# Product 5 of the first layer split into seven products of its blocks, in a routed expert kernel

## The chip, the cores and the metric

The kernel runs on one core of a Trainium2 chip. The metric is the time of one execution on the device in microseconds (us), as the median of several runs.

## The reference, cut to what matters

A token mixture with eight experts. `x` has 4096 tokens of 512 numbers. Each token is rotated by a fixed 4 x 4 mixing of its four quarters (a product of two normalized quaternions and a spectral gate, which here only scales), routed to its two best experts, and each expert takes up to 1024 tokens:

```python
de = disp.reshape(E, cap, Dm)                                   # E = 8, cap = 1024, Dm = 512
h = jax.nn.relu(jnp.einsum('ecd,ehd->ech', de, fc1_w) + fc1_b)  # H = 2048
eo = jnp.einsum('ech,ehd->ecd', h, fc2_w) + fc2_b
gathered = eo.reshape(E * cap, Dm)[flat_idx]
out = jnp.sum(gathered * (gates * w)[:, :, None], axis=1)
x = x + out                                                     # added to the input
```

All arithmetic of the two layers is in float32.

## The kernel before, in words

**Stages.** A routing stage computes the choice of experts and the slot tables (about the first 45 us). Then the experts follow, each in four groups of 512 hidden units: group k is quarter g = k mod 4 of expert e = k div 4, so there are 32 groups.

**First layer.** Each group is a product of a 512 x 512 block of w1 with the expert's 512 x 1024 rotated inputs. Both factors are halved in both directions, and the product is formed in Winograd's form of Strassen's scheme, with seven products, numbered 0 to 6, instead of eight. The sums of w1's blocks are made on GpSimd (`left1`, lines 137 to 140: s0 to s3), those of the inputs once per expert, also on GpSimd (`sums`, lines 125 to 128, tiles x0 to x3). Factor 5 on the left is s1, factor 4 is s0, factor 2 is s3.

Products 1, 2, 3, 4 and 6 are split a second time in the same form: `left_sub` makes four more 128 x 128 sums on GpSimd for each of them and each group (lines 155 to 158, tiles sub), `right_sub` four more on VectorE for each of them and each expert (lines 170 to 173, tiles xsub). `within` (line 840) is one matmul of 128 x 128 with 256 columns on one such block; a product takes seven. Products 0 and 5 are not split: `half` (line 861) uses two matmuls of 512 columns for each half m, so a product takes four. A float32 matmul is two instructions in the profile.

Results land in PSUM banks (`bank1`, four of them in rotation) and are added by VectorE into four SBUF tiles, h11, h22, h21 and r12, which lie side by side in `beside`. A block that is wanted in two outputs is added to both at once. ACT copies the first results with the bias and applies the final relu. The last block of the chain is closed by `chain`: three sums of these tiles on VectorE at once (lines 827 to 829) and a fourth (`last`, line 824) as soon as product 2 of the group before has freed its tile.

**Second layer.** One step behind, the hidden units of the group before are multiplied with w2 in the same seven-product form, once for each pair of slot tiles (`st0` 0 and 2); `product2` (line 800) is eight instructions of 256 columns. VectorE adds each into the accumulator `acc` (lines 1239 to 1291); the first sum of each goes to a tile v1 of its own pool. GpSimd makes w2's sums (`right2`, tiles t).

**Order.** Nothing is scheduled automatically: the instructions stand in each engine's queue in the order in which the Python code emits them. The first layer is a generator that yields 14 times in a group, the second one also 14 times, and the driver takes one step of each in turn, so that a step of the first layer stands between two of the second on TensorE. The step number within the group, `i`, is called turn here. At each turn the driver emits further work: `later(steps, turns)` puts sums at given turns, `TURN_OF_SUM` the four sums s of the next group's weights (s2 at turn 8, s0 at 11, s1 at 12, s3 at 13), `fill_n` the four x sums of the next expert at turns 10 to 13 of g = 3. Two lists hold work without a fixed turn: `background` (VectorE's rotation of the next expert's inputs, lines 727 and 771; the stores of a finished expert, which are an ACT scaling, a GpSimd addition, line 673, and a scatter, line 657) and `fetches` (gathers on GpSimd's queue, lines 601, 633 and 694, and the exchanges of gathered inputs on SP's queue, line 707). The table `PACE` says how many of each are emitted after each step.

**Buffers that matter here.** The tiles s0 to s3 and the sub tiles exist once: the sum for the next group can be written only when TensorE has done the last matmul that reads the old one. GpSimd works strictly in its queue's order, and so do VectorE and TensorE's matmuls.

**Start.** The output is first filled with x by a DMA of 8 MB from ACT's queue (line 1155), during group 0; the expert results are later gathered from it, added to, and scattered back. Group 0 has a plain first layer without the seven-product form.

## Time and profile before

| | |
|---|---|
| median of 3 runs | 1560.28 us (1560.1 to 1561.2) |
| profiled execution | 1562.67 us, span of the trace 1560.9 us |
| TensorE matmul busy | 1522.0 us, 98% |
| VectorE busy | 1237.8 us, 79% |
| GpSimd busy | 1105.4 us, 71% |
| ACT busy | 332.0 us, 21% |
| mean granted TensorE clock | 0.987 |

The span runs from the first to the last instruction of the profiled execution. In the rows of the trace, PE is TensorE's matmuls, PEld its weight loads, DVE VectorE, POOL GpSimd, SPq the DMA queue of SyncE. A row in order of time has its start, its duration, engine, line, operation, output and inputs, shape and count; in brackets, how long the engine was idle before it and what ended that. TensorE's matmuls overlap, so that the time of one is best read from start to start.

### The profile page before, as it was taken

Reading aid. Unit: us, or ns where it says so; the run is one execution under the profiler, and the core shown is the slowest. Engines: PE = TensorE matmul, PEld = TensorE weight load, DVE = VectorE, ACT = ScalarE, POOL = GpSimd, SP = SyncE. Lnnn points to the kernel's source line nnn. Section 1 sums busy time; section 2 is a strip of 40 time slices with the busy share of each in tenths; the row PEclk is TensorE's granted clock in tenths of the full one; section 3 lists DMA queues with packets and bytes.
Section 4 is the critical chain, followed back from the end, with each engine's and each line's share of the span. In section 5 each row is a group of like instructions: output and inputs, shape, how many; then the busy total and the mean of one; then the engine's idle time right before and its main releaser. Section 6 shows DMA issues by size and latency. Waiting matters only on the chain.

```text
span 1560.9 us, 18187 instructions
## 1 busy us (share of the span) xinstructions
PE 1522.0 (98%) x6585; PEld 1220.2 (78%) x6585; DVE 1237.8 (79%) x1733; ACT 332.0 (21%) x477; POOL 1105.4 (71%) x1253
## 2 busy tenths in 40 slices
PE   5898999999999999999999999999999999999997
PEld 3676888877778878788887778887777887888886
DVE  6586888788977888688896889878898788866656
ACT  3221212221122211221113121222112221121110
POOL 1755678857898379984799567885778847987453
PEclk7899999999999999999999999999999999999999
DMA  8463104521235113440145210452123511321021
GB/s 326 159 214 94 55 28 142 148 68 55 74 115 161 36 55 113 133 140 28 38 132 157 86 54 28 142 149 68 55 70 113 142 58 55 113 96 67 1 81 53
DMA packets 79378, 152.23 MB, mean 98 GB/s; under 512 B 12022, under 2 KB 40950, under 8 KB 74168
## 3 DMA queue, kind: packets, MB, share of 16 engines
q1 hardware_dynamic: 56848, 90.24, 18.3%
q0 software_dynamic: 18048, 52.31, 11.1%
q10 hardware_dynamic: 4392, 8.52, 1.4%
q8 instruction: 52, 0.85, 0.2%
q14 instruction: 38, 0.31, 0.1%
HBM read 119.77 MB, written 25.23 MB: 93 GB/s over the span
## 4 chain that ended last, share of the span: by engine, by line
PE 88%; DVE 5%; DMA 2%; SPq 2%; POOL 1%; another core or an unknown queue 1%; issue 1%; POOLq 0%; DVEq 0%
PE a L800 26%; PE b L800 20%; PE t L840 17%; PE a L861 13%; PE u L840 7%; PE b L840 3%; PE a L840 2%; DMA xb<-in_xt_dram 1%; SPq L707 1%; PE p L992 1%; DVE xsub L173 1%; DVE beside L891 1%; DVE beside L901 0%; DMA xa<-in_xq_dram,slot_tok 0%
## 5 line engine op out<-in xcount | busy, mean ns | idle before, releaser
L836 ACT ACTIVATE beside<-beside 128x1024 f32<-128x1024 f32 x93 | 98.4, 1058 | 727.9 <-DVE beside L891 507.8
L800 PE MATMUL a<-t,beside 128*128 128x256 f32 x1024 | 242.0, 379 | 0.1
L800 PEld LDWEIGHTS a<-t,beside 128*128 128x128 f32 x1024 | 194.5, 190 | 39.7 <-issue 14.4
L891 DVE TENSOR_TENSOR beside<-t,beside 128x512 f32<-128x512 f32 x248 | 170.4, 687 | 68.9 <-PE t L840 57.3
L840 PE MATMUL t<-xsub,sub 128*128 128x256 f32 x682 | 180.0, 383 | 0.9 <-DVE beside L891 0.8
L840 PEld LDWEIGHTS t<-xsub,sub 128*128 128x128 f32 x682 | 126.8, 190 | 24.3 <-DVE beside L901 4.5
L861 PE MATMUL a<-x,s 128*128 128x512 f32 x248 | 118.4, 600 | 5.1 <-POOL s L138 5.1
L800 PE MATMUL b<-w,beside 128*128 128x256 f32 x512 | 121.0, 379 | 0.6 <-DVE acc L1284 0.6
L800 PE MATMUL a<-t,hidden 128*128 128x256 f32 x512 | 121.0, 379 | 0.0
L800 PE MATMUL a<-w,beside 128*128 128x256 f32 x512 | 120.9, 379 | 0.0
L800 PE MATMUL b<-w,hidden 128*128 128x256 f32 x504 | 119.7, 380 | 0.0
L800 PE MATMUL b<-t,hidden 128*128 128x256 f32 x504 | 119.1, 379 | 0.0
L800 PEld LDWEIGHTS b<-w,beside 128*128 128x128 f32 x512 | 97.2, 190 | 27.3 <-issue 15.8
L800 PEld LDWEIGHTS a<-w,beside 128*128 128x128 f32 x512 | 97.3, 190 | 26.4 <-issue 14.8
L800 PEld LDWEIGHTS b<-w,hidden 128*128 128x128 f32 x504 | 96.3, 191 | 26.5 <-issue 13.2
L861 PE MATMUL a<-xa,w 128*128 128x512 f32 x248 | 116.4, 592 | 0.0
L137 POOL TENSOR_TENSOR s<-w 128x512 f32<-128x512 f32 x31 | 39.5, 1276 | 106.7 <-PE t L840 106.7
L800 PEld LDWEIGHTS a<-t,hidden 128*128 128x128 f32 x512 | 97.3, 190 | 13.2
L800 PEld LDWEIGHTS b<-t,hidden 128*128 128x128 f32 x504 | 95.8, 190 | 13.0
L901 DVE TENSOR_TENSOR beside<-t,beside 128x512 f32<-128x512 f32 x124 | 85.1, 686 | 17.5 <-PE t L840 13.8
L657 POOL DMA_INDIRECT out_dram<-rows,slot_add x64 | 71.4, 1116 | 36.9 <-DVE rows L652 17.5
L140 POOL TENSOR_TENSOR s<-w,s 128x512 f32<-128x512 f32 x31 | 40.3, 1299 | 66.8 <-PE t L840 66.6
(231 smaller groups left out, 3178.5 us busy)
## 6 DMA issues: line engine op xcount, KB each, us to landing
w<-in_w_dram SPq DMA_DIRECT2D x64, 1024.0 KB
xb<-in_xt_dram SPq DMA_DIRECT2D x8, 1024.0 KB
out_dram<-in_x_dram ACTq DMA_DIRECT2D x1, 8192.0 KB
rows<-xa SPq DMA_DIRECT2D x112, 64.0 KB
rows<-xb SPq DMA_DIRECT2D x224, 32.0 KB
b<-in_b_dram POOLq DMA_DIRECT2D x8, 256.0 KB
c<-choice,slot_cho POOLq DMA_INDIRECT x64
rows<-out_dram,slot_tok POOLq DMA_INDIRECT x64
```

Source lines behind the costliest of these rows:

```text
L137: lambda: G.tensor_tensor(s[0], w[:, 1, 0], w[:, 1, 1], ALU.add),
L140: lambda: G.tensor_tensor(s[3], w[:, 0, 1], s[1], ALU.subtract),
L173: lambda: V.tensor_tensor(t[:, 3], b(1, 0), t[:, 1], ALU.subtract),
L657: nc.gpsimd.indirect_dma_start(out=out_of[st], out_offset=bass.IndirectOffsetOnAxis(ap=slot_add[:, s : s + 1], axis=0), in_=self.rows[st], ...
L707: nc.sync.dma_start(slots_of[half][q * CW : (q + 1) * CW, at : at + t.shape[1], b * P : (b + 1) * P], t[b * CW : (b + 1) * CW, :, q * P : ...
L800: nc.tensor.matmul(out[m] if isinstance(out, list) else out[:, m], lhsT=factors[0][n][:, c, (st0 + m) * P : (st0 + m + 1) * P], rhs=factor ...
L836: nc.scalar.activation(h, h, AF.Relu)
L840: nc.tensor.matmul(out, lhsT=subs[0][n][i], rhs=subs[1][n][i], start=first, stop=True, skip_group_check=True,)
L861: nc.tensor.matmul(out, lhsT=factors[0][n][:, c, m * P : (m + 1) * P], rhs=factors[1][n][:, c, :], start=first and c == 0, stop=c == 1, sk ...
L891: V.tensor_tensor(to, bank.rearrange("p (n s) -> p n s", n=2), to, ALU.add)
L901: V.tensor_tensor(to, term.unsqueeze(1).to_broadcast([P, 2, HS]), to, ALU.add)
L992: nc.tensor.matmul(ps[n][m][:, at], lhsT=w[:, block, i // 2, i % 2, m * P : (m + 1) * P], rhs=x.of(half, i)[:, at], start=i == 0 and at.st ...
```

## The change

Product 5 is split like the others. Its seven block products have four turns to themselves (3 to 6, with the start in turn 2), and their results are added by VectorE to r12 alone: four blocks to one place each, one block to two. h21, which holds r12's values with another bias, is then carried over: half 0 as the sum of product 6's block, the bias difference `b1_over` and r12 on VectorE, half 1 by ACT from r12. All later steps move on by one or two turns, products 1 and 4 overlap, and the turns for the sums and the table PACE are set anew. The sums of product 5 and product 4 on the left share one tile (sub4). The tile v1 is given up: its sum goes to a part of `acc`. The 8 MB copy to the output is issued at group 1, turn 13.

```diff
-    def left_sub(k, n, block):
+    def left_sub(k, n, block, tag=None):
...
-        t = wsum.tile([P, 4, P], F32, tag=f"sub{n}", name=f"sub{n}_{k}")
+        t = wsum.tile([P, 4, P], F32, tag=f"sub{tag or n}", name=f"sub{n}_{k}")
...
+    b1_over = const.tile([P, E, NG, 2], F32, name="b1_over")
+    by_half = b1_sb.rearrange("p e (g a m) -> p e g a m", a=2, m=2)
+    nc.gpsimd.tensor_tensor(b1_over, by_half[:, :, :, 1], by_half[:, :, :, 0], ALU.subtract)
...
-        for m in range(2):
-            half(a[m], m, 5, False)
-            nc.scalar.activation(r12[:, m], a[m], AF.Identity, bias=lo[:, m : m + 1])
             if m == 1:
-                nc.scalar.activation(h21[:, m], a[m], AF.Identity, bias=hi[:, m : m + 1])
+                nc.scalar.activation(r12[:, m], a[m], AF.Identity, bias=lo[:, m : m + 1])
...
+        t5 = bank1(f"t5_{k}")
+        singles(a[0], 5)
+        nc.scalar.activation(r12[:, 0], a[0], AF.Identity, bias=lo[:, 0:1])
+        within(t5[:, A], subs, 5, 0, True)
+        yield
+        within(t5[:, B], subs, 5, 4)
+        add_once(r12[:, 0, A], t5[:, A])
+        yield
+        within(t5[:, A], subs, 5, 5)
+        add_once(r12[:, 0, B], t5[:, A])
+        add_once(r12[:, :, B], t5[:, B].unsqueeze(1).to_broadcast([P, 2, HS]))
+        yield
+
+        u = bank1(f"u1_{k}")
+        within(t5[:, A], subs, 5, 6)
+        add_once(r12[:, 1, B], t5[:, A])
+        singles(u, 6, True)
+        V.scalar_tensor_tensor(h21[:, 0], u, over[:, 0:1], r12[:, 0], ALU.add, ALU.add)
+        yield
+        t = bank1(f"t1_{k}")
+        within(t5[:, A], subs, 5, 3)
+        add_once(r12[:, 1, A], t5[:, A])
+        nc.scalar.activation(h21[:, 1], r12[:, 1], AF.Identity, bias=over[:, 1:2])
...
             if k:
+                lefts[5], more = left_sub(k, 5, left_f[5], 4)
+                later(more, (0, 0, 1, 1))
                 for n, block, turns in (
-                    (4, left_f[4], (2, 2, 3, 3)),
-                    (2, left_f[2], (4, 4, 5, 5)),
-                    (3, w1_of[k][:, 1, 1], (6, 6, 7, 7)),
+                    (2, left_f[2], (2, 2, 3, 4)),
+                    (3, w1_of[k][:, 1, 1], (6, 7, 7, 8)),
                 ):
...
                     for n, turns in (
-                        (6, (2, 2, 3, 3)),
-                        (4, (3, 4, 4, 5)),
-                        (2, (2, 4, 7, 10)),
-                        (3, (3, 5, 8, 10)),
+                        (5, (1, 2, 3, 4)),
+                        (6, (4, 5, 5, 7)),
+                        (4, (7, 7, 9, 9)),
+                        (2, (7, 8, 9, 11)),
+                        (3, (8, 9, 11, 12)),
                     ):
...
+                    if i == 5:
+                        its[4], more = left_sub(k, 4, left_f[4])
+                        later(more, (5, 5, 6, 6))
...
+                if k == 1 and i == 13:
+
                     nc.scalar.dma_start(*(a.rearrange("(b r) d -> r b d", r=PT) for a in (out, x)))
...
-            v1 = vp.tile([P, 2, DB], F32, tag="v", name=f"v1_{k}_{st0}")
+            v1 = accs[st0][:, :2, :DB]
...
         [(1, 1)] * 2 + [(1, 1)] * 4 + [(0, 0)] + [(0, 1)] * 5 + [(1, 1), (0, 0)],
-        [(1, 1)] * 4 + [(1, 2), (0, 2), (0, 0), (0, 1), (0, 1), (0, 0), (1, 1), (0, 0), (1, 1), (0, 0)],
-        [(1, 1)] * 2 + [(2, 1)] * 2 + [(1, 2), (1, 1), (0, 0), (0, 1), (0, 1), (0, 0), (1, 1), (0, 0), (1, 1), (0, 0)],
-        [(1, 1)] * 6 + [(0, 0)] + [(0, 1)] * 4 + [(1, 2), (1, 2), (1, 1)],
+        [(1, 1)] * 4 + [(0, 0), (1, 2), (0, 0), (1, 1), (0, 1), (1, 1), (0, 0), (0, 1), (2, 1), (0, 1)],
+        [(1, 1)] * 2
+        + [(1, 2), (0, 1), (0, 0), (1, 2), (0, 0), (1, 1), (0, 1), (1, 1), (0, 0), (0, 1), (2, 1), (0, 1)],
     )
```

The first row of PACE (g = 0) is as it was. GpSimd's queue in the new program has, where g = 0 passes into g = 1: s0, a store, s1, a store, s3, the four steps of sub5, then three of w2's sums.

More of the change, by code (lines that the diff above doesn't have):

```diff
@@ L577 @@
     hp = ctx.enter_context(tc.tile_pool(name="hp", bufs=1))
-    vp = ctx.enter_context(tc.tile_pool(name="vp", bufs=1))
     xdp = ctx.enter_context(tc.tile_pool(name="xdp", bufs=2))
@@ L853, in layer1 @@
         lo, hi = (b1_sb[:, e, g * 4 + 2 * a : g * 4 + 2 * a + 2] for a in range(2))
+        over = b1_over[:, e, g]
         h = beside[k % 2]
@@ L872, in layer1 @@
             nc.scalar.activation(h11[:, m], a[m], AF.Identity, bias=lo[:, m : m + 1])
-            yield
-        for m in range(2):
-            half(a[m], m, 5, False)
-            nc.scalar.activation(r12[:, m], a[m], AF.Identity, bias=lo[:, m : m + 1])
             if m == 1:
-                nc.scalar.activation(h21[:, m], a[m], AF.Identity, bias=hi[:, m : m + 1])
+                nc.scalar.activation(r12[:, m], a[m], AF.Identity, bias=lo[:, m : m + 1])
             yield
@@ L896, in add_twice, with add_once @@
             V.tensor_tensor(to, term, to, ALU.add)
+        def add_once(to, term):
+            V.tensor_tensor(to, term, to, ALU.add)
         def add_to_both(two, m, half, term):
@@ L901, in add_to_both, with add_twice_to_both @@
             V.tensor_tensor(to, term.unsqueeze(1).to_broadcast([P, 2, HS]), to, ALU.add)
+        def add_twice_to_both(two, term):
+            to = two[:, :, :, B]
+            term = term.unsqueeze(1).unsqueeze(1).to_broadcast([P, 2, 2, HS])
+            V.tensor_tensor(to, term, to, ALU.add)
         def add_pair(one, bank):
             V.tensor_tensor(one[:, 0], bank, one[:, 0], ALU.add)
-        two = h[:, 0:3:2]
-        t, u = bank1(f"t1_{k}"), bank1(f"u1_{k}")
-        singles(a[0], 6)
-        nc.scalar.activation(h21[:, 0], a[0], AF.Identity, bias=hi[:, 0:1])
+        two, three, four = h[:, 0:3:2], h[:, 2:4], h[:, 1:4:2]
+        t5 = bank1(f"t5_{k}")
[20 more added lines that the diff above has]
+        nc.scalar.activation(h21[:, 1], r12[:, 1], AF.Identity, bias=over[:, 1:2])
         both(t, 1, 6, 0, True)
@@ L919, in layer1 @@
         yield
+        b, t4 = bank1(f"b_{k}"), bank1(f"t4_{k}")
         both(t, 1, 6, 6)
@@ L923, in layer1 @@
         add_pair(h11, u)
+        singles(b, 4, True)
+        V.tensor_tensor(h22[:, 0], b, h21[:, 0], ALU.add)
+        within(t4[:, A], subs, 4, 0, True)
+        add_to_both(four, 0, A, t4[:, A])
         yield
@@ L927, in layer1 @@
         relu(h11)
-        yield
         nc.scalar.activation(h22[:, 1], h21[:, 1], AF.Copy)
-        two = h[:, 1:4:2]
-        b, t4 = bank1(f"b_{k}"), bank1(f"t4_{k}")
-        singles(b, 4, True)
-        V.tensor_tensor(h22[:, 0], b, h21[:, 0], ALU.add)
-        within(t4[:, A], subs, 4, 0, True)
-        add_to_both(two, 0, A, t4[:, A])
-        yield
         within(t4[:, A], subs, 4, 5)
         within(t4[:, B], subs, 4, 4)
-        add_to_both(two, 0, B, t4[:, A])
-        to = two[:, :, :, B]
-        term = t4[:, B].unsqueeze(1).unsqueeze(1).to_broadcast([P, 2, 2, HS])
-        V.tensor_tensor(to, term, to, ALU.add)
+        add_to_both(four, 0, B, t4[:, A])
         yield
-        three = h[:, 2:4]
         t, u = bank1(f"t3_{k}"), bank1(f"u3_{k}")
         singles(b, 2)
-        within(t4[:, A], subs, 4, 6)
-        add_to_both(two, 1, B, t4[:, A])
+        add_twice_to_both(four, t4[:, B])
         both(t, 3, 2, 0, True)
@@ L952, in layer1 @@
         yield
-        within(t4[:, A], subs, 4, 3)
-        add_to_both(two, 1, A, t4[:, A])
-        relu(h22)
+        within(t4[:, A], subs, 4, 6)
+        add_to_both(four, 1, B, t4[:, A])
         both(t, 3, 2, 5)
@@ L960, in layer1 @@
         yield
+        within(t4[:, A], subs, 4, 3)
+        add_to_both(four, 1, A, t4[:, A])
+        relu(h22)
         both(t, 3, 2, 6)
@@ L1125, in first_layers @@
                     right_subs[1], more = right_sub(xtp, e, 1, xf[1])
-                    later(more, (0, 0, 1, 1))
-                units = layer1(k, (left_f, xf), (dict(lefts), right_subs))
+                    later(more, (2, 3, 4, 5))
+                its = dict(lefts)
+                units = layer1(k, (left_f, xf), (its, right_subs))
             else:
@@ L1142, in first_layers @@
                             later(more, turns)
-                        if g == NG - 1:
-                            right_subs[1], more = right_sub(xtp, e + 1, 1, xf_n[1])
-                            later(more, (10, 12, 12, 13))
+                    if i == 9 and k + 1 < NK and g == NG - 1:
+                        right_subs[1], more = right_sub(xtp, e + 1, 1, xf_n[1])
+                        later(more, (11, 12, 12, 13))
+                    if i == 5:
+                        its[4], more = left_sub(k, 4, left_f[4])
+                        later(more, (5, 5, 6, 6))
                     for f in ahead[i]:
@@ L1159, in first_layers @@
                         fetches.extend(nxt.arrive(*part))
-                    if (g, i) in (((1, 7), (2, 6)) if e else ((1, 11), (2, 6))):
+                    if (g, i) in ((1, 7), (2, 6)):
                         background.extend(nxt.steps(g - 1))
@@ L1204, in start @@
             e, g = divmod(k, NG)
-            before = biases[e] if g == 0 else accs[st0]
+            if g == 0:
+                before = biases[e]
+                accs[st0] = ap.tile([P, 4, D], F32, tag=f"acc{st0}", name=f"acc{st0}_{e}")
+            else:
+                before = accs[st0]
             a = banks(f"a2_{k}_{st0}", (k, st0) == units[-1])
-            v1 = vp.tile([P, 2, DB], F32, tag="v", name=f"v1_{k}_{st0}")
+            v1 = accs[st0][:, :2, :DB]
             product2(a, st0, (hidden[k], rights[k]), 0, True)
@@ L1216, in second_layers @@
             e, g = divmod(k, NG)
-            if g == 0:
-                before = biases[e]
-                acc = accs[st0] = ap.tile([P, 4, D], F32, tag=f"acc{st0}", name=f"acc{st0}_{e}")
-            else:
-                before = acc = accs[st0]
+            acc = accs[st0]
+            before = biases[e] if g == 0 else acc
             factors = (hidden[k], rights[k])
@@ L1323 @@
                 k, i = now
-                turn(1 if k in (0, NK - 1) else PACE[3 if k == 1 else min(k % NG, 2)][i][n])
+                turn(1 if k in (0, NK - 1) else PACE[min(k % NG, 2)][i][n])
         while background:
```

## The prediction

> **What bounds the kernel now.** I read the page first, then the busy time of three whole groups, then TensorE and GpSimd in order of time around a group's start. [...]

> ```profile
> PE 1522.0 (98%) x6585; PEld 1220.2 (78%) x6585; DVE 1237.8 (79%) x1733; ACT 332.0 (21%) x477; POOL 1105.4 (71%) x1253
> ...
> PE 88%; DVE 5%; DMA 2%; SPq 2%; POOL 1%; another core or an unknown queue 1%; issue 1%; POOLq 0%; DVEq 0%
> ```

> TensorE is the bound, and waits for almost nothing. But 71% for GpSimd is a mean over unlike groups:

> ```profile
> 409.08:455.56 46.48, 46.41 (x200) 37.52 (x199) 39.63 (x57) 10.26 (x15) 42.14 (x47) 1.00 0.45 137
> 455.56:501.74 46.18, 46.18 (x200) 37.54 (x198) 32.68 (x41) 12.56 (x19) 38.59 (x46) 1.00 0.46 129
> 501.74:547.90 46.16, 46.16 (x199) 37.19 (x198) 39.39 (x52) 9.92 (x15) 22.19 (x28) 1.00 0.19 56
> ```

> The columns are the stretch, its length, then PE, PEld, DVE, ACT, POOL. These are k = 8, 9, 10 (g = 0, 1, 2). In g = 0 GpSimd is busy 42.14 of 46.48 us, and the rest is gaps of 0.15 to 0.3 us around its DMA issues: it is full. It carries the old expert's stores and the next one's gathers there. How late it runs shows where it passes from g = 0 to g = 1:

> ```profile
> 454.31 1.29 POOL L137 TENSOR_TENSOR s<-w 128x512 f32<-128x512 f32 x1
> 455.54 1.29 POOL L673 TENSOR_TENSOR rows<-acc,rows 128x512 f32<-128x512 f32 x1
> 457.11 1.01 POOL L657 DMA_INDIRECT out_dram<-rows,slot_add  x1 [0.28 <-POOL rows L673]
> 458.14 1.35 POOL L138 TENSOR_TENSOR s<-s,w 128x512 f32<-128x512 f32 x1
> 459.45 1.26 POOL L673 TENSOR_TENSOR rows<-acc,rows 128x512 f32<-128x512 f32 x1
> 460.99 1.68 POOL L657 DMA_INDIRECT out_dram<-rows,slot_add  x1 [0.28 <-POOL rows L673]
> 462.68 1.38 POOL L140 TENSOR_TENSOR s<-w,s 128x512 f32<-128x512 f32 x1
> ```
> ```profile
> 455.56 1.88 PE L861 MATMUL a<-xa,w 128*128 128x512 f32 x4
> 459.00 1.88 PE L861 MATMUL a<-xa,w 128*128 128x512 f32 x4
> 462.44 1.88 PE L861 MATMUL a<-x,s 128*128 128x512 f32 x4
> ```

> Product 5 of k = 9 starts at 462.44 and reads s1 (L138), complete at 459.5: about 3 us to spare. s3 (L140) comes only at 464.06, 1.62 us after that start. Over k = 5, 9, 13, 17, 21, 25 these 1.62 us are 2.63, 1.62, 1.62, 1.61, 1.64, 3.17, sum 12.3.

> **The change, part by part.**

> *TensorE.* Product 5 was 4 matmuls of 512 columns, now 7 of 256. Eight second-layer instructions of 256 columns stand 1.73 us apart, 0.216 each; a matmul is two instructions. One matmul of 256 columns less is 0.432 us, in 31 groups **-13.4 us**. All of it is on the path.

> *Output's copy.* It was issued at 57.7 us. SP's exchanges waited 13.2 us for it, GpSimd 24.0 us for an exchange, and so TensorE for GpSimd:

> ```profile
> 128.59 1.89 PE L800 MATMUL a<-t,beside 128*128 128x256 f32 x8
> 135.62 3.78 PE L861 MATMUL a<-x,s 128*128 128x512 f32 x4 [5.13 <-POOL s L138]
> 139.19 2.49 PE L800 MATMUL b<-w,hidden 128*128 128x256 f32 x8
> ```

> 5.13 us idle, and then slow matmuls: 3.57 us to the next start instead of 1.72, and 2.32 instead of 1.72, 2.45 in all. Issued at k = 1, turn 13, the copy is behind these exchanges: **-7.6 us**. Its 8 MB then run beside loads of w1 and w2 not wanted for a group; before it moved some 205 GB/s, so 40 us, and the first row gather from the output comes at 244 us. Nothing for that.

> *GpSimd, k = 1.* sub5's four steps come among the four gathers after the x sums, which end at 80.0. Three gathers at 1.27, two steps at 0.43, a gather, two steps end at 87.0; TensorE asks at 80.30 + 3.44 + 0.43 = 84.2: +3 us. VectorE, with four more xsub steps there, +1. **+4 us**.

> *GpSimd, g = 0 into g = 1.* This is the term that decides. Against the 1.62 us by which s3's end follows the start of turn 2, four shifts:
> 1. The order is now s1, a store, s3, then all four steps of sub5, and turn 2's second matmul reads the last one. Four steps at 0.42 to 0.46: +1.75.
> 2. k = 8 has its own sub5 in the same full queue, some steps beside VectorE: +1.85.
> 3. The run starts later. s0 waits for product 4's last matmul (block 3), which moves from turn 11 to turn 12:

> ```profile
> 399.15 0.59 PE L840 MATMUL t<-xsub,s 128*128 128x256 f32 x2
> ...
> 409.08 1.88 PE L861 MATMUL a<-xa,w 128*128 128x512 f32 x4
> ```
> ```profile
> 399.82 1.27 POOL L137 TENSOR_TENSOR s<-w 128x512 f32<-128x512 f32 x1 [5.65 <-PE t L840]
> ```

> s0 started 9.26 us before the group's first matmul. Now 28 instructions lie between that read's end and the group: 28 x 0.216 = 6.05, less 0.25 for the end and start, so 5.8. The shift is +3.46, less a wait of 0.71 that s3 had and loses: +2.75.
> 4. TensorE is 0.43 earlier by its saving, and asks 0.43 later, for the second matmul: 0.

> So 1.62 + 6.35 = 8.0 us late. Over six experts 12.3 + 6 x 6.35 = **+50.4 us**. Nothing hides it: TensorE is in order, and all before the wait has been done. Part of it (about 1.3) should fall at turn 8 of g = 0, where sub4, moved behind the gathers and into sub5's buffer, is also wanted; the queue is one, so the sum stays. The last expert has no gathers: k = 29 comes out about even.

> The price of a step: groups of sub rows average 0.47 to 0.70, single ones 0.45 with 0.42 from start to start. [...] I take 0.45; the means would make it 2.4 a sub5, 7 us more over six experts, kept for the range.

> *The clock after each wait.* The row: 5.13 us idle cost 2.45. [...] By the row alone six waits are 14.7 us. [...]

> *VectorE.* New per group: four adds of 256 (0.42 by the small SBUF rows), one of 512 (0.69), and h21's sum with the bias (0.74); the second product-6 read from ACT goes. That is 3.1 us; a group of 39.4 goes to 42.5 of 45.7, still under. But turn 4 overwrites the half bank that turn 2 wrote, so it needs the first of the new adds, and that one stands behind three others:

> ```profile
> 512.27 0.69 DVE L1291 TENSOR_TENSOR acc<-b,acc 128x512 f32<-128x512 f32 x1 [0.67 <-PE b L800]
> 512.88 1.22 DVE L824 TENSOR_TENSOR hidden<-beside,hidden 128x1024 f32<-128x1024 f32 x1
> 514.01 1.40 DVE L771 SCALAR_TENSOR_TENSOR xa<-xps,M,xa 128x512 f32<-128x512 f32 x2
> ```

> From the end of turn 2's second-layer product: 0.2 + 0.61 + 1.13 + 0.67 + 0.42 = 3.0 us, against 0.43 + 1.73 = 2.16 on TensorE: 0.9 late in g = 2 and 3, where an xa step stands between (14 groups, 12.6 us); 0.25 in those without. In g = 0 and 1 it disappears in the wait for GpSimd. **+13 us**; ends 3 (adds ahead of these products) and 22 (L824 at its 2.24 beside GpSimd).

> *The rest.* v1 in acc's tile instead of its own: same add, same order, 0. ACT: one PSUM read fewer; at 21%, nothing. b1_over: one small sum at the start, 0. SP's queue: no load moves past another but the copy.

> **Sum**: -13.4 - 7.6 + 4 + 50.4 + 11 + 13 = +57.4. The profiled execution took 1562.67 (span 1560.9, 1.8 around it): 1620.1. It stands 2.4 above the median 1560.28: **1617.7**, say 1618.

> **The rivals.**

> *GpSimd's lateness is absorbed* (faster). If sub5 is ready before turn 2 of g = 1, the sum keeps -13.4 - 7.6 + 4 and perhaps 5 of VectorE's term: -12, 1548; with VectorE's at nothing 1543. For it: GpSimd idles 24 of 46 us in g = 2, so the work fits on average. Against: the queue is static, and between 411 and 484 us it has no gap to give. The point is the lateness at that turn: with VectorE's +13 it must stay under 0.7 us, with +5 under 2, where I find 8.0. 0.13.

> *Only the queue's delay* (slower, less). The clock holds and VectorE keeps up: 1560.3 - 17 + 50.4 = 1594. For it: VectorE's slack elsewhere in the trace. Against: the row at 135.62. 0.17.

> *VectorE becomes the bound.* Each turn from 3 to 6 pays, 2 us a group: 62 instead of 13, 1667. g = 2 is near it; but the adds' starts, 0.61 apart, leave room. 0.07.

> *It doesn't do what it says*: the instructions' order shows seven matmuls for product 5 in every group from k = 1, so no chance of note.

> **How the numbers follow.** The likeliest case has 0.63; its bounds (clock 0 to 14.7, VectorE 3 to 22, sub5 at the means) give 1597 to 1637. The range takes in the smaller case too, there with 6 us instead of 8 a pair (1580), and above a second wait of about 1 us in each pair, for sub4 in g = 1 (1643): 1580 to 1645. Faster by over 0.2% (about 3 us, what a measurement can tell): 0.13; within: 0.03; slower: 0.84.

> **What would show it.** In the profile after: a wait of TensorE for sub's last step (L158) of 5 to 8 us in k = 5, 9, ..., 25, and slow matmuls behind it; a wait of 0.5 to 1 us for VectorE's add into r12 in g = 2 and 3; no wait at k = 2 for s1. Groups g = 2, 3 of about 46.6 us and g = 0 with 1 of about 101 together confirm it; g = 0 with 1 at 92 would refute it.

## The result, and the profile after

The changed kernel takes 1661.99 us (median of 5 runs, 1659.05 to 1663.08) where the kernel before takes 1560.10 beside it (5 runs, 1558.85 to 1561.20): a ratio of 1.065, 95% interval 1.0636 to 1.0667. The forecast was 1618, with a range up to 1645. The direction and the first place of the loss (the wait for sub5's last step) are right, the size is not: 102 us are lost instead of 57.

The page of the changed kernel, busy times and the chain that ended last:

```profile
PE 1540.7 (93%) x6771; PEld 1261.3 (76%) x6771; DVE 1354.6 (82%) x1951; ACT 312.7 (19%) x446; POOL 1169.5 (71%) x1378
...
PE 48%; POOL 31%; DVE 9%; issue 7%; DMA 2%; SPq 2%; ACT 1%; POOLq 0%; DVEq 0%; ACTq 0%
```

TensorE's share of the chain fell from 88% to 48%, and GpSimd holds 31% where it held 1%, though it is busy 71% of the span as before. Its mean load says nothing here; its place does. The waits of TensorE (us in total, times, longest) are almost all new:

```profile
PE a L843 <- POOL sub L158: 42.8, 15, 4.2
PE t L843 <- DVE beside L899: 24.4, 35, 1.2
PE t L843 <- DVE beside L891: 11.3, 20, 1.0
```

L899 is the add of t5 into r12, L891 the add of a pair of block products. The first row is the foreseen wait for sub5's last step, but it comes 15 times, not six: once at k = 1, then at turn 2 of every g = 0 (2.6 us, seven times) and of every g = 1 from k = 5 to 25 (3.4 us, six times), and 0.2 at k = 29. The forecast had one wait of up to 8 us in each pair. The other two rows are VectorE, 35.7 us where the forecast had 13. The four groups of one expert (stretch, length, then busy us of PE, PEld, DVE, ACT, POOL, granted clock, DMA share, GB/s), k = 8 to 11:

```profile
426.11:479.29 53.18, 48.72 (x205) 39.37 (x204) 45.11 (x68) 10.41 (x14) 47.85 (x53) 0.97 0.38 121
479.29:531.92 52.63, 48.20 (x205) 39.70 (x204) 40.24 (x50) 11.67 (x18) 40.89 (x49) 0.97 0.43 119
531.92:579.68 47.76, 46.35 (x206) 38.51 (x205) 41.66 (x58) 9.56 (x14) 24.13 (x33) 1.00 0.16 50
579.68:626.62 46.94, 46.16 (x206) 38.56 (x204) 41.82 (x56) 6.53 (x9) 35.95 (x42) 1.00 0.14 45
```

Against 46.48, 46.18, 46.37 and 46.39 before. In g = 0 and 1 the granted clock is 0.97 instead of 1.00. Each wait, and what follows it, in TensorE's rows of k = 8 and 9:

```profile
436.20 0.70 PE L843 MATMUL a<-x,sub 128*128 128x256 f32 x2 [2.60 <-POOL sub L158]
436.73 0.92 PE L843 MATMUL t<-x,s 128*128 128x256 f32 x2
437.44 3.30 PE L803 MATMUL b<-w,hidden 128*128 128x256 f32 x8
...
490.16 0.70 PE L843 MATMUL a<-x,sub 128*128 128x256 f32 x2 [3.39 <-POOL sub L158]
490.70 0.59 PE L843 MATMUL t<-x,s 128*128 128x256 f32 x2
491.13 3.27 PE L803 MATMUL b<-w,hidden 128*128 128x256 f32 x8
```

Eight second-layer instructions that stand 1.73 us apart elsewhere take 3.14 and 3.06 to the next start: waits of 2.60 and 3.39 us each cost some 1.6 to 1.8 us more in slow matmuls. And GpSimd, around the wait of k = 9:

```profile
481.94 1.27 POOL L676 TENSOR_TENSOR rows<-acc,rows 128x512 f32<-128x512 f32 x1
483.49 1.70 POOL L660 DMA_INDIRECT out_dram<-rows,slot_add  x1 [0.28 <-POOL rows L676]
485.19 1.30 POOL L140 TENSOR_TENSOR s<-w,s 128x512 f32<-128x512 f32 x1
486.41 1.47 POOL L155 TENSOR_TENSOR sub<-s 128x128 f32<-128x128 f32 x1
487.96 1.32 POOL L156 TENSOR_TENSOR sub<-sub,s 128x128 f32<-128x128 f32 x1
489.25 0.45 POOL L157 TENSOR_TENSOR sub<-s 128x128 f32<-128x128 f32 x1
489.66 0.45 POOL L158 TENSOR_TENSOR sub<-s,sub 128x128 f32<-128x128 f32 x1
```

The order is the one forecast: a store, s3, sub5. But two of the four small steps take 1.3 to 1.5 us instead of 0.45. VectorE runs its chain of hidden sums just then (L831 from 484.83, L832 from 487.50). In k = 8 it is three of the four:

```profile
431.51 1.43 POOL L155 TENSOR_TENSOR sub<-s 128x128 f32<-128x128 f32 x1
433.01 1.32 POOL L156 TENSOR_TENSOR sub<-sub,s 128x128 f32<-128x128 f32 x1
434.30 0.45 POOL L157 TENSOR_TENSOR sub<-s 128x128 f32<-128x128 f32 x1
434.71 1.43 POOL L158 TENSOR_TENSOR sub<-s,sub 128x128 f32<-128x128 f32 x1
```

### The profile page after: what moved, and what is told of

The parts are those of the page before. It is cut to its first block, busy times and chain, and to the rows that moved or that the text cites. A ratio compares the mean times of both kernels' runs of the same rounds, so it can differ in the third digit from the quotient of the medians.

```text
span 1657.2 us, 18908 instructions
## 1 busy us (share of the span) xinstructions
PE 1540.7 (93%) x6771; PEld 1261.3 (76%) x6771; DVE 1354.6 (82%) x1951; ACT 312.7 (19%) x446; POOL 1169.5 (71%) x1378
## 4 chain that ended last, share of the span: by engine, by line
PE 48%; POOL 31%; DVE 9%; issue 7%; DMA 2%; SPq 2%; ACT 1%; POOLq 0%; DVEq 0%; ACTq 0%
PE a L803 16%; PE t L843 12%; PE b L803 8%; PE u L843 5%; PE a L865 3%; POOL rows L676 3%; POOL rows L600 3%; POOL sub L155 3%; POOL out_dram L660 3%; POOL sub L156 2%; POOL sub L158 2%; POOL sub L157 2%; DVE hidden L827 2%; POOL xa L697 2%; SPq L710 1%
## 5 line engine op out<-in xcount | busy, mean ns | idle before, releaser
L843 PE MATMUL t<-xsub,sub 128*128 128x256 f32 x868 | 239.4, 388 | 39.6 <-DVE beside L899 24.4
L843 PEld LDWEIGHTS t<-xsub,sub 128*128 128x128 f32 x868 | 158.4, 190 | 88.6 <-DVE beside L899 43.3
L891 DVE TENSOR_TENSOR beside<-t,beside 128x512 f32<-128x512 f32 x248 | 170.1, 686 | 32.0 <-PE t L843 26.2
L803 PE MATMUL b<-w,hidden 128*128 128x256 f32 x504 | 130.5, 406 | 0.0
L137 POOL TENSOR_TENSOR s<-w 128x512 f32<-128x512 f32 x31 | 39.5, 1275 | 123.8 <-PE t L843 123.8
L803 PEld LDWEIGHTS b<-w,hidden 128*128 128x128 f32 x504 | 104.1, 206 | 16.7
L803 PEld LDWEIGHTS a<-t,hidden 128*128 128x128 f32 x512 | 97.3, 190 | 13.2
L1321 DVE TENSOR_TENSOR acc<-b,acc 128x512 f32<-128x512 f32 x63 | 43.5, 690 | 78.0 <-PE b L803 78.0
L155 POOL TENSOR_TENSOR sub<-s 128x128 f32<-128x128 f32 x124 | 76.5, 617 | 38.1 <-PE t L843 38.0
```

The lines of the kernel that those rows point to most:

```text
L137: lambda: G.tensor_tensor(s[0], w[:, 1, 0], w[:, 1, 1], ALU.add),
L155: lambda: G.tensor_tensor(t[:, 0], b(1, 0), b(1, 1), ALU.add),
L803: nc.tensor.matmul(out[m] if isinstance(out, list) else out[:, m], lhsT=factors[0][n][:, c, (st0 + m) * P : (st0 + m + 1) * P], rhs=factor ...
L843: nc.tensor.matmul(out, lhsT=subs[0][n][i], rhs=subs[1][n][i], start=first, stop=True, skip_group_check=True,)
L891: V.tensor_tensor(to, bank.rearrange("p (n s) -> p n s", n=2), to, ALU.add)
L1321: V.tensor_tensor(o12, b, o12, ALU.add)
```

## Experiments

Each run's time stands against its own runs of the kernel before (1559.6 to 1561.7).

### Copy alone

In the kernel before:

```diff
+                if k == 1 and i == 13:
                     nc.scalar.dma_start(*(a.rearrange("(b r) d -> r b d", r=PT) for a in (out, x)))
```

> The kernel before, with one part of the change alone: output's copy issued at k = 1, turn 13, instead of k = 0, turn 1. Theory: the stall at 128 to 142 us goes, and nothing else moves: 1560.1 - 7.6 = 1552.5, with k = 2 at about 46.3 us instead of 53.9. Rival: the 8 MB of the copy now run beside the loads of w1 and w2 and delay one of them, so that k = 2 or 3 waits for a weight: 1558 or more.

Measured: 1553.58 against 1559.64, ratio 0.9960 (0.9946 to 0.9974). k = 2 takes 46.18 us instead of 53.94, and k = 3 is unchanged (46.32 after 46.31): the theory holds, no weight is delayed. In this profile k = 1 started 0.9 us later, in the part that the edit does not touch. This part of the change alone is faster than both kernels.

### Which of the two suspects

Three runs: product 5 reading raw blocks of s1, with sub5's steps gone; the five adds of t5 gone; both gone.

```diff
-                lefts[5], more = left_sub(k, 5, left_f[5], 4)
-                later(more, (0, 0, 1, 1))
+                s5 = left_f[5]
+                lefts[5] = [s5[:, c, m * P : (m + 1) * P] for m, c in ...]
```
```diff
-        add_once(r12[:, 0, A], t5[:, A])
-        add_once(r12[:, 0, B], t5[:, A])
-        add_once(r12[:, :, B], t5[:, B].unsqueeze(1).to_broadcast([P, 2, HS]))
-        add_once(r12[:, 1, B], t5[:, A])
-        add_once(r12[:, 1, A], t5[:, A])
```

> The changed kernel without sub5's four GpSimd steps in each group: product 5 reads the raw blocks of s1 in their place (the sums of its left blocks are left out). Theory (GpSimd's queue and the slow clock behind its waits are about 10 us a pair of groups g = 0, 1): the waits for L158 at turn 2 go in all seven experts, and k = 1 gets some 4 us shorter: 1662 - 7 x 9 - 4 = about 1595; g = 0 and 1 come to about 49 and 48 us. Rival (VectorE is the larger part, and its waits grow into the freed time): not under 1625, with g = 0 and 1 still above 50.

> The changed kernel without VectorE's five adds of t5 into r12 in each group (product 5's block sums are computed on TensorE and not added). Theory (VectorE's waits at turns 4, 5, 11 and 12 are 1.2 to 2.9 us in every group, some 7.5 an expert): 1662 - 55 = about 1607, g = 2 and 3 at 45.8 us. Rival (the prediction's size, 0.9 us in g = 2 and 3 alone): 1649, with the waits of g = 0 and 1 unchanged.

> Both left out: sub5's steps and the adds of t5 into r12. Theory (the two account for the whole of the loss, and add up): 1560.1 - 13.4 (matmuls) - 7.6 (copy) = about 1539, groups of 45.8 us throughout. Rival (a third cost is hidden behind the two, as in the longer series of xsub sums on VectorE in g = 0 and k = 1, or later s0): 1550 or more, with g = 0 above 47.

Measured: 1630.7, 1635.8 and 1611.6. Sub5 is worth 31 us instead of 67, the adds 26 instead of 55, both together 50 instead of 123. All three theories missed; the rivals of the first (but for 49.9 in g = 1) and of the third came true. Length of a group, in us:

| kernel | k = 1 | g = 0 (k = 8) | g = 1 (k = 9) | g = 2 | g = 3 |
|---|---|---|---|---|---|
| before | 43.13 | 46.48 | 46.18 | 46.37 | 46.39 |
| changed | 50.90 | 53.18 | 52.63 | 47.76 | 46.94 |
| without sub5 | 44.72 | 51.49 | 49.86 | 47.87 | 46.91 |
| without adds | 51.96 | 51.49 | 52.24 | 46.60 | 45.74 |
| without either | 47.30 | 51.38 | 50.19 | 46.60 | 45.74 |

In g = 2 and 3 the adds are the whole of VectorE's cost but 0.86 us in g = 2. With them gone g = 3 shows what a group takes without waits: 45.74, against 46.15 for the kernel before (k = 29), so the matmul saved is worth 0.41. In g = 0 and 1, 5.6 and 4.4 us stay with both suspects gone. The waits without sub5 tell that another took sub5's place; L170 is the first of VectorE's four sums of product 5's right blocks, L1317 an add of the second layer:

```profile
PE t L843 <- DVE beside L899: 18.8, 28, 1.1
PE t L843 <- DVE xsub L170: 16.2, 7, 2.3
PE b L803 <- DVE acc L1317: 11.8, 7, 1.9
```

Both wait for VectorE. Why VectorE is late shows in the rows without either, at the start of k = 9 (464.86): VectorE, then GpSimd in the same stretch.

```profile
466.40 3.49 DVE L830 SCALAR_TENSOR_TENSOR hidden<-beside 128x1024 f32<-128x1024 f32 x1
469.81 0.68 DVE L1228 TENSOR_TENSOR acc<-a,b 128x512 f32<-128x512 f32 x1
470.42 3.98 DVE L831 TENSOR_TENSOR hidden<-hidden,beside 128x1024 f32<-128x1024 f32 x1
474.32 2.28 DVE L832 SCALAR_TENSOR_TENSOR beside<-beside 128x1024 f32<-128x1024 f32 x1
476.52 0.68 DVE L1312 TENSOR_TENSOR acc<-a,acc 128x512 f32<-128x512 f32 x1
```
```profile
466.29 1.29 POOL L138 TENSOR_TENSOR s<-s,w 128x512 f32<-128x512 f32 x1
467.52 1.28 POOL L676 TENSOR_TENSOR rows<-acc,rows 128x512 f32<-128x512 f32 x1
469.08 1.69 POOL L660 DMA_INDIRECT out_dram<-rows,slot_add  x1 [0.28 <-POOL rows L676]
470.78 1.30 POOL L140 TENSOR_TENSOR s<-w,s 128x512 f32<-128x512 f32 x1
472.01 1.30 POOL L125 TENSOR_TENSOR t<-w 128x512 f32<-128x512 f32 x1
473.38 2.14 POOL L126 TENSOR_TENSOR t<-w,t 128x512 f32<-128x512 f32 x1
475.48 2.25 POOL L127 TENSOR_TENSOR t<-w 128x512 f32<-128x512 f32 x1
```

A sum of the chain takes 1.22 us alone (L831 at two places of the changed kernel where GpSimd has no sum). L830 takes 3.49: it ends 1.1 us after GpSimd's second sum is over, so by these rows it stood still beside two of them. L831 spans s3 and the first t sum. The chain needs 10 us from 466.40 to 476.52, and only then comes L1312, an add of the second layer for which TensorE waits 1.89 us.

### The third suspect: sums that hold each other up

On the kernel without either: without VectorE's right sums of product 5 as well, or without GpSimd's four t sums.

```diff
-                rights[k + 1], more = right2(k + 1, loaded[k + 1])
+                rights[k + 1] = [w2_next_k[:, c, :, h * DB : (h + 1) * DB] for c, h in ...]
+                more = [lambda: None] * 4
```

> As the run without sub5's steps and without the adds of t5 (1611.6), and VectorE's four sums of product 5's right blocks are left out too (raw blocks are read in their place). Theory (in g = 0 TensorE now needs VectorE as early as turn 3, where its chain of four hidden sums still runs): the wait for L170 of 2.3 us in g = 0 goes with the 1.9 us of slow matmuls behind it, g = 1 stays at 50.2: 1611.6 - 7 x 4.2 = about 1582. Rival (the late chain itself is what is waited for): the wait turns up at the next bank of the second layer, as in g = 1, and g = 0 stays above 49: 1600.

> As the run without sub5's steps and without the adds of t5 (1611.6), and GpSimd's four t sums of each group's second layer are left out too (raw blocks of w2 are read in their place); VectorE's work is the same. Theory (sums with two SBUF operands on GpSimd and VectorE hold each other up, and at the start of g = 0 and 1 GpSimd issues them without a gap): VectorE's chain L830 to L832 falls from 2.2 to 2.6 us a sum to 1.3 to 1.7, g = 0 and 1 from 51.3 and 50.2 to about 47.5: 1611.6 - 7 x 3.8 - 6 x 2.7 = about 1569. Rival (VectorE's load or order alone): the chain's times stay and so do the groups, 1605 or more.

Measured: 1601.5 and 1560.4. Without the right sums g = 0 fell to 49.2 only, and TensorE's waits for the second layer's add went from 7 (12.4 us) to 14 (22.2 us): the rival, the chain is late whoever asks for it. Without the t sums 51 us went (forecast 43): k = 8 takes 47.23 us, k = 9 46.48. VectorE's work is the same, its durations are not. GpSimd's shorter queue alone does not explain it: with the t sums TensorE waits in g = 0 and 1 for GpSimd 3.7 us and for VectorE 36.0, without them 0.2 and 6.1. The chain in groups (busy us, mean ns), first with the t sums, then without:

```profile
L830 DVE SCALAR_TENSOR_TENSOR hidden<-beside 128x1024 f32<-128x1024 f32 x32 | 83.3, 2604 | 8.4 <-ACT beside L1023 8.3
L831 DVE TENSOR_TENSOR hidden<-hidden,beside 128x1024 f32<-128x1024 f32 x32 | 77.9, 2434 | 0.8
L832 DVE SCALAR_TENSOR_TENSOR beside<-beside 128x1024 f32<-128x1024 f32 x32 | 52.8, 1650 | 0.0
```
```profile
L830 DVE SCALAR_TENSOR_TENSOR hidden<-beside 128x1024 f32<-128x1024 f32 x32 | 69.0, 2156 | 8.4 <-ACT beside L1023 8.3
L831 DVE TENSOR_TENSOR hidden<-hidden,beside 128x1024 f32<-128x1024 f32 x32 | 51.6, 1613 | 0.8
L832 DVE SCALAR_TENSOR_TENSOR beside<-beside 128x1024 f32<-128x1024 f32 x32 | 41.7, 1304 | 0.0
```

The size was forecast too low for L830 (2.2 us, not 1.7): its neighbours are s1 and a store, not the t sums.

Two runs then asked whether the t sums act in the changed kernel itself, and whether the kernel before pays for them.

> The changed kernel, complete on VectorE's side and with sub5, but without GpSimd's four t sums of each group (raw blocks of w2 are read in their place). Theory (GpSimd's and VectorE's two-operand sums hold each other up at the start of g = 0 and 1, and sub5 stands in that crowd): g = 0 and 1 fall from 53.2 and 52.6 to about 48.5, sub5's steps in k = 8 take 2 us instead of 4.6, g = 2 and 3 lose a part of their turn-4 wait: 1662 - 7 x 4.7 - 6 x 4.1 - 5 = about 1600. Rival (the queue's order alone: the t sums stand behind sub5 and so delay nothing at turn 2): the waits for L158 stay, 1645 or more.

> The control: the kernel before with output's copy moved (1553.6), without GpSimd's four t sums. Theory (before the change the same sums stood there, VectorE's chain was somewhat slowed by them, and no instruction of TensorE waited for it): groups of 46.2 to 46.5 fall to 46.15 at best, 1553.6 - 5 = about 1549. Rival (the sums cost the kernel before as much as the changed one): 1500.

Measured: 1642.9 and 1550.1. The control holds: before the change the t sums cost 3.5 us, and among the groups g = 0 alone shows it (46.15 instead of 46.47). The first theory missed, 19 us instead of 62; its rival was right about the wait and 2 us too high in the time. The waits for L158 are the same to the tenth, 42.8 us in 15, and sub5's four steps in k = 8 still take 4.6 us (1.43, 1.32, 0.45, 1.43). So in the changed kernel the t sums, which stand behind sub5, do not make sub5 late; what stands ahead of it and beside it does. What goes is VectorE's share: waits for L899 fall from 24.4 to 11.6 us. The t sums matter more when sub5 is taken out, for then they move up beside the chain (L125 and L126 beside L831 in the rows above). So the loss behind sub5 and the loss behind the t sums stand in for each other. That this is why taking sub5 away gave half of what its wait had shown is argued from these rows; no run leaves out sub5 and the t sums with the adds in place.

### Can order mend it?

Four runs with the same work in another order: VectorE's adds; sub5 ahead of s3; the row gathers in g = 3; all three. The edits of the first three, cut:

```diff
         within(t5[:, A], subs, 5, 0, True)
+        add_once(r12[:, 0, A], t5[:, A])
         yield
         within(t5[:, B], subs, 5, 4)
-        add_once(r12[:, 0, A], t5[:, A])
...
-        add_twice_to_both(four, t4[:, B])
         both(t, 3, 2, 0, True)
-        add_pair(r12, b)
         add(three, 0, A, t)
+        add_pair(r12, b)
+        add_twice_to_both(four, t4[:, B])
```
```diff
-                lefts[5], more = left_sub(k, 5, left_f[5], 4)
-                later(more, (0, 0, 1, 1))
+                if k == 1:
+                    lefts[5], more = left_sub(k, 5, left_f[5], 4)
+                    later(more, (0, 0, 1, 1))
...
+                if k and left_n and i == 13:
+                    lefts[5], more = left_sub(k + 1, 5, left_n[5], 4)
+                    for f in more:
+                        f()
```
```diff
+            if g == 2 and st0 == 2 and e + 1 < E:
+                fetches.extend(lambda st=st, r=rows[e]: r.gather_rows(st) for st in STORED)
...
-            if g == (NG - 1 if e + 1 < E else 2) and st0 == 0:
+            if e + 1 == E and g == 2 and st0 == 0:
```

> The changed kernel with VectorE's order altered at two places: product 5's first add into r12 is issued in turn 2 instead of turn 3 (ahead of the second layer's adds), and in turn 10 the add of t stands ahead of the two sums that nobody waits for. Same work. Theory (the waits of TensorE for L899 and L891 come from the order in VectorE's queue, not from its load): g = 2 and 3 fall from 47.8 and 46.9 to 45.8 each, 22 us over the run, and with some of it in g = 0 and 1 about 1632. Rival (VectorE's load is the cause): the waits turn up at the next instruction, g = 2 stays above 47, 1650 or more.

> The changed kernel with sub5's four steps issued in turn 13 of the group before, behind s1 and ahead of s3 and the last x sum. Same work. Theory (the order in GpSimd's queue makes L158 late): in g = 0 sub5 is done some 4 us earlier and its wait with the slow matmuls (4.5 us) goes; in g = 1 1.3 us earlier, so about 2 of 5.3 go: 1662 - 7 x 4.5 - 6 x 2 = about 1618. Rival (GpSimd's and VectorE's sums hold each other up at the start of g = 0 and 1, as the runs without sub5 hint: there g = 0 and 1 still took 51.5 and 50): another wait takes its place, at 1640 or more.

> The changed kernel with the eight gathers of output rows (L600, about 1.25 us each) issued in g = 3, from the middle of the group on, instead of g = 0. Same work, 10 us less in GpSimd's queue in g = 0. Theory (the full queue of g = 0 makes g = 1 late): g = 1's wait for L158 and the slow matmuls behind it (5.3 us) go, g = 0's stay: 1662 - 6 x 5 = about 1630. Rival (the queue waits at s0 for TensorE's turn 12 in any case, and the stores that follow stay between s1 and sub5): g = 1 gains under 2 us, 1650.

> The three alterations together: adds first, sub5's steps first, row gathers in g = 3. Same work as the changed kernel. Theory (queue order is all of the loss beyond k = 1): g = 0 and 1 at about 47 us, g = 2 and 3 at 45.8: 1560.1 - 21 + 8 + 7 x 2.5 = about 1565. Rival (sums with two SBUF operands on GpSimd and VectorE hold each other up, a loss that order does not remove): g = 0 and 1 still at 49 to 51, 1600.

Measured: 1675.5, 1661.5, 1686.0 and 1698.6; no theory came true in its time, and the rivals of the first two did. TensorE's waits with the adds first, then with sub5 first:

```profile
PE t L843 <- DVE beside L909: 35.2, 31, 2.3
PE a L843 <- POOL sub L158: 31.8, 15, 4.0
PE t L843 <- DVE beside L899: 19.6, 21, 1.9
```
```profile
PE t L843 <- DVE beside L899: 31.6, 36, 1.4
PE b L843 <- POOL sub L158: 15.7, 7, 3.7
PE a L843 <- POOL sub L158: 15.5, 7, 4.2
PE t L843 <- DVE xsub L170: 11.4, 7, 1.6
```

With the adds first, the wait of g = 2 left turn 4 and came back at turn 5 (0.57 us, L899), and the sum put behind (L909, reading one half of a bank) held up the matmul that writes the other half in turn 11: g = 2 and 3 at 47.9 and 48.0. With sub5 first, its wait in turn 2 went from g = 0 and fell from 3.4 to 1.9 us in g = 1, as that theory has it. In their place sub4 came up to 3.7 us late at turn 8 of g = 1 ("b" in the second row), VectorE's right sums up to 1.6 us late in g = 0, and g = 0 stayed at 52.5. With the gathers in g = 3, g = 1 fell to 48.6 as the queue's theory wants, but the gathers now stood among the x sums, ahead of sub5 in g = 0, and that wait went to 9.45 us (g = 0 at 60 us). All three together: a new wait for the t sums, 29.9 us in 7.

A last pair moved the background's steps of g = 2 and 3 to turns 5 to 13, L909 to turn 9 and k = 1's sub5 into k = 0; and used the new product 5 in g = 2 and 3 alone, with the old turns elsewhere. Of the first edit the table PACE is shown, of the second the choice of the first layer; the second also issues VectorE's right sums of product 5 in g = 1 and alters PACE once more.

```diff
-        [(1, 1)] * 2
-        + [(1, 2), (0, 1), (0, 0), (1, 2), (0, 0), (1, 1), (0, 1), (1, 1), (0, 0), (0, 1), (2, 1), (0, 1)],
+        [(1, 1), (1, 0), (0, 1), (0, 0), (0, 0), (1, 2), (1, 1)]
+        + [(1, 1), (1, 1), (1, 1), (0, 0), (0, 1), (2, 1), (1, 1)],
```
```diff
+                split = g > 1
...
+                units = (layer1 if split else layer1_whole5)(k, (left_f, xf), (its, right_subs))
```

> The changed kernel with three alterations in separate groups, same work. (1) g = 2, 3: the background's steps (the next expert's x) are taken in turns 5 to 13 instead of 0 to 5. (2) The sum of t4's second half (L909) is issued in turn 9, where VectorE idles, instead of turn 10. (3) k = 1: sub5's steps are issued in k = 0, where GpSimd idles, instead of between the gathers. Theory (VectorE is short only in turns 2 to 5, and the waits at turns 4 and 11 are a matter of which work stands there): g = 2 and 3 at 45.8 us each, k = 1 at 45 instead of 50.9: 1662 - 7 x 3.1 - 6 = about 1634. Rival (its load in the whole group is too much): the waits move to later turns, g = 2 above 47, and only k = 1 gains: 1655.

> A mixture: product 5 by its own seven blocks only in g = 2 and 3, with the pacing of the run before this one; in g = 0 and 1 (and k = 1) product 5 whole and the turns and pacing of the kernel before; output's copy at k = 1, turn 13. Same result by other sums. Theory (the change costs only where GpSimd is full, and its saving of 0.43 us a group, with a wait of about 0.2 that the kernel before has in these groups, comes out where it is not): g = 0 and 1 as before at 46.5 and 46.2, g = 2 and 3 at 45.8 instead of 46.4: 1553.6 - 15 x 0.6 = about 1545. Rival (VectorE's five more adds in g = 2 and 3 fill the chain's turns again, or sub5 makes GpSimd late in g = 0 through g = 3's end): 1554 or more.

Measured: 1664.8 and 1604.6. In the first, k = 1 fell from 50.9 to 46.8 and g = 2 from 47.8 to 46.9, as wished in part; g = 3 stayed (46.9), g = 1 fell to between 47.4 and 49.2 from k = 9 on, and g = 0 rose to between 58 and 60 in k = 8 to 24, with new waits of 2 us for VectorE at later turns (L891, L173 in k = 8). In the second, none of the groups gained: 50.1, 47.3, 48.3 and 47.5 in k = 8 to 11, above the kernel before in each. Why its g = 2 is 0.5 us over even the changed kernel's was not taken apart. No order tried here beats the kernel before; with the copy alone moved, 1553.6 stays the best.

## Why the prediction was right or wrong

Point by point, in us. The waits are the bracketed ones in TensorE's rows, added up for k from 2 on; lengths of groups are taken over 45.74.

| step | forecast | measured |
|---|---|---|
| one matmul less in 31 groups | -13.4 | -12.8 (0.41 a group) |
| copy moved | -7.6 | -6.1; k = 2 alone -7.8 |
| k = 1 | +4 | +8.6 (50.90 against 42.70 - 0.41) |
| waits for GpSimd, g = 0 and 1 | +50.4 | +41.2 |
| slow matmuls behind them | +11 | +14.7 (nine stretches of 1.4 to 1.8) |
| waits for VectorE, g = 0 and 1 | 0 | +21.8 |
| rest of g = 0 and 1 | not named | +15.2 |
| VectorE, g = 2 and 3 | +13 | +22.9 |

The measured column adds up to 105.5; less the 0.2 to 0.3 us by which groups of the kernel before exceed 46.15 (about 5.5 in all) it is 100, for 102. The rest of g = 0 and 1 is 92.8 us over 14 groups less the three rows above it. A stop takes longer than its bracket: at 436.20 TensorE starts 2.77 us later than unhindered, where the bracket has 2.60, and g = 3, with one wait of 0.78, is 1.20 longer than 45.74. At 0.17 to 0.42 us each, the 58 waits of g = 0 and 1 would make 10 to 24 us of it (an estimate), so the rest need not have a further cause; what it is made of was not shown.

- *TensorE and the copy* were right, the second by a run of its own.
- *The queue* came out a fifth too high, and its working was wrong. It fell in two pieces, 2.6 us in g = 0 and 3.4 in g = 1, and the last expert, forecast about even, waits 2.6 in its g = 0 too. The later start (shift 3) shows at k = 8: s0 stands 5.80 us ahead of the group's first matmul, just as forecast, and s3 ends 3.13 us after it instead of 0.14 before. But shifts 2 and 3 did not reach k = 9. There s3 ends 7.19 us after the group's first matmul, where the kernel before has 8.50 and the forecast some 13, because k = 8 itself took 6.7 us longer and GpSimd caught up in it. "The queue is one, so the sum stays" is the step that failed here. In its place stand sub5's own steps, put at 1.75 us: four took 4.6 in k = 8 and 3.7 in k = 9, beside VectorE's chain. At 1.75 sub5 of k = 8 would have ended at 433.3, before TensorE asked for it (433.6), and k = 9 would have waited about 1.4 us instead of 3.39 (estimates from the rows above). That two errors nearly cancel in the sum is luck.
- *VectorE* is the step that failed worst. The prediction said "In g = 0 and 1 it disappears in the wait for GpSimd"; 21.8 us did not. TensorE's wait gives VectorE time, but its chain, slowed by GpSimd's sums, used that up: turn 4 waits 0.92 us in k = 8, after 0.79 in g = 2. Without the t sums 7.2 of the 21.8 us were left. In g = 2 and 3 the turn-4 term was about right (0.79 and 0.78 for 0.9), and a second wait at turn 11 (L891 behind L909, 0.62) was not seen.
- *The clock* came out near in size, by luck: no run shows the term of 11 us that stands for it in the sum. What the runs showed in its place is 14.7 us in nine stretches. All thirteen waits of g = 0 and 1 are between 2.58 and 3.39 us; behind nine of them the clock was at 0.50, behind four it stayed at 1.00. In the trace of the changed kernel the clock changes on a fixed raster of 3.41 us, and a step of it need not be idle to have half clock behind it: in front of the ten half-clock steps in k = 1 to 30 (one in k = 1, nine in g = 0 and 1) TensorE was busy for 13 to 39% of one. The row at 135.62, a price for each wait, was near enough to count by, though four of thirteen waits cost nothing and nine cost 1.4 to 1.8 us instead of 2.45; by it a wait split in two can pay twice.
- *k = 1*: the wait was put at 3 us and measured 4.24. The gathers were taken at 1.27 each; in the rows of the kernel before these four take 6.85 together (80.17 to 87.02). Not counted were a step at half clock behind the wait and 1.8 us for VectorE in turn 11. With sub5 moved out of the gathers 4.1 came back, without sub5 6.2.
- *The sum as such* was wrong in form. It added the delays of two engines as if they were independent. Removing sub5 gave 31 us and removing the adds 26, nearly the 50 that both gave together; but with both removed 67 us stayed in g = 0 and 1, and it took the t sums, which the change does not touch and which cost the kernel before 3.5 us, to bring that to 16.
- A small misreading: the third stretch shown in the prediction ends at 547.90, 0.21 us before k = 11 starts; k = 10 takes 46.37 us, not 46.16.

The rivals: absorption is refuted by 15 waits. "Only the queue's delay" is refuted by the slow matmuls and VectorE's rows. "VectorE becomes the bound, 1667" gives nearly the time, but by luck: it let turns 3 to 6 pay 2 us in every group on top of the forecast's GpSimd term. Of VectorE's waits in g = 2 and 3 it has the size in g = 2 (2.0, and 1.2 in g = 3) but not the turns, which are 4 and 11, and 0.86 of g = 2's stayed when the adds were gone.

What stays open: which sum of the kernel should move so that g = 0 and 1 keep their old spacing with sub5 in them. Four orders did not find it.

## What to carry to other kernels

Before adding work to an engine, look at what it runs beside: two engines whose sums with two SBUF operands delay each other (here L831 took 2434 ns a sum with the t sums beside it, 1613 without) are one resource in that stretch, and the mean load of neither shows it. Cost a stretch in which both are full as one queue (a rule of thumb that fits these runs and was not tried as a forecast), and expect that the wait removed gives way to the next; take away both suspects at once, and a third that was there before. A wait on the bound engine also gives the others time to catch up (s3 of k = 9 ended 7.19 us after its group's first matmul, not the forecast 13), so a lag doesn't simply carry over into the next stage. A new wait of TensorE can be paid for again in matmuls at half clock: here 37 of 52 waits of 1.5 us or more had them behind, and the nine in g = 0 and 1 of the changed kernel lost 1.4 to 1.8 us each by it.

## What the runs showed of the hardware

```profile
433.46:436.87 3.41, 0.81 (x4) 0.62 (x4) 3.41 (x5) 0.00 (x0) 3.41 (x4) 1.00 0.00 0
436.87:440.28 3.41, 3.41 (x10) 2.70 (x9) 0.96 (x2) 0.69 (x1) 3.33 (x4) 0.50 0.00 0
634.84:638.25 3.41, 1.55 (x7) 1.40 (x8) 3.41 (x5) 0.69 (x1) 3.33 (x4) 1.00 0.00 0
638.25:641.66 3.41, 3.41 (x17) 2.70 (x15) 2.16 (x3) 0.00 (x0) 3.41 (x3) 1.00 0.20 35
```

The first wait lies inside one step, which has 0.81 us of TensorE's work in it, and the next step is at 0.50. The second is cut by a border, 1.55 us of work are left in the step, and the next one is at 1.00. Over all sixteen traces, without the first 60 and the last 8 us, a step at full clock in which TensorE was busy under 42% was followed by one at half in 85 of 85 cases, between 42 and 48% in 20 of 44, above that in none of 7013; in the traces of the kernel before and the changed one alone it is 11 of 11, none of 4 and none of 872. By these counts a wait had half clock behind it here if it took about 1.9 us out of one step (an estimate: 3.41 less 45%). In the kernel before, the changed one and three experiments (without sub5, without either, gathers in g = 3), 37 of 52 waits from 1.5 us up had half clock behind them (10 of 14 in the changed kernel), and their length says little: 1.87 us could be enough, and one of 3.39 passed without.
- *A sum on VectorE was held off through two sums of GpSimd at some places, but mostly got its turn after one.* This is read from the ends of the rows. Where no sum of GpSimd runs beside it, L831 takes 1.22 us in the changed kernel (two places), beside such sums 1.36 to 2.75. The adds with an operand in PSUM show nothing of the kind: L891 takes 0.67 to 0.69 at all 248 places there, beside GpSimd's sums or not. In the rows without either above, L830 took 3.49 us, begun 0.11 us after s1: it was held off through s1 and through the store's sum behind it as well, for the last 1.22 us of its row begin about where that sum ends (468.80). L831 was passed over in the same way between s3 and the first t sum, though its row begins at 470.42, 0.36 us before that of s3: it ends 1.09 us after the t sum. L832, the next one, waited for L126 alone: it ends 1.08 us after L126, and L127, which stood behind L126 without a gap, took 2.25 us instead of 1.27. In that run (without either) a sum of the chain waited at 105 places where two sums of GpSimd stand back to back (within 0.1 us); it came in between them at 92 and was passed over at 13, always between s1 and the store (6) or between s3 and the first t sum (7). The same count gives 107 and 6 in the changed kernel, all six between s1 and the store. What decides it stays open.
